# A different passage between two layers of one kernel, and a different order of its beginning

## The chip, the cores and the metric

The kernel runs on one core of a Trainium2 chip. The core has TensorE (PE, matrix products; the loads of its stationary operand are listed as PEld), VectorE (DVE), ScalarE (ACT), GpSimd (POOL) and SyncE (SP), which here only issues transfers. Each engine works through its own instructions in their order and waits for others through semaphores. Sixteen DMA engines move data between the memory outside (HBM) and the core's SBUF. TensorE writes to PSUM, from which VectorE and ScalarE read. The metric is the device time of one execution, in microseconds, and the median of several runs.

## The reference

Two residual layers over `x` of 8 batches, 1024 positions and 512 channels, in float32. The first is attention with weights that are scaled by a condition, the second a gated scan over the positions.

```python
# layer 0: attention
x = x * s1[:, None, :]                                  # s1, s2: halves of the condition
x = (x - mu) * jax.lax.rsqrt(var + EPS_IN)              # over the 512 channels
dcoef = lambda w, s: jax.lax.rsqrt(jnp.einsum('oi,bi->bo', jnp.square(w), jnp.square(s)) + EPS_DM)
q, k, v = (x @ w.T * dcoef(w, s1))                      # v times s2 as well; 16 heads of 32
attn = softmax(q @ k.T * d ** -0.5) @ v
x1 = x_in + attn @ w_weight.T * w_dc + v_flat @ u_weight.T * u_dc
# layer 1: gated scan
xr, gate = jnp.split(x1 @ W_in.T, 2, axis=-1)           # 1024 channels each
xc = silu(conv4(xr + t_emb) + b_conv)                   # along the positions
xn = (xc - mu) / jnp.sqrt(var + 1e-05) * ln_g + ln_b
Bm, Cm, dt = jnp.split(xn @ W_xproj.T, 3, axis=-1)      # 16 states
dt = jnp.tanh(dt @ W_dt.T + b_dt) * 0.01
Ad = 1.0 + dt * A
Bd = Bm * jnp.minimum(norm(xn), 1.0)
h = clip(h * ad + bd * xt, -10, 10);  yt = ct @ h       # 1024 steps, one after the other
out = x1 + (ys + D * xn) * silu(gate) @ W_out.T
```

## The kernel before

The kernel has two functions that run one after the other, and the order of the instructions is written out by hand.

`modulated_attention` first loads and normalises the first batch in two halves of 512 positions (`load_x`, L62; `normalise`, L75 to L89: GpSimd multiplies by the condition and applies mean and deviation, VectorE takes the statistics) and turns it by TensorE transposes so that channels lie on the partitions (`turn`, L99, into tiles `xh`). It then computes the five demodulations: load a weight matrix (L121), square it (L122), multiply by the squared condition in 16 small products per matrix with the weights as the stationary operand (L127), take root and reciprocal (L135, L136). Then `project` computes q, k and v for the first 128 output channels (four heads). A `chain` (L156) is four matrix products that add up in one PSUM tile, and `project` has six of them and two groups of transposes (L202). Copies of q and k shifted by 64 partitions are made by DMA on SP (`moved`, L180 and L181).

The main loop runs over 32 blocks (8 batches of 4 groups of four heads) and in each over 16 slots (8 tiles of 128 queries by 2 pairs of heads). A slot issues: scores (L255, L258), their maxima on VectorE (L363), transposes of the slot before's probabilities (`flip`, L265), exponentials on ScalarE (L373), normalisation on GpSimd (L378, L387, L392), copies out of PSUM, and in every second slot the product with v (`weigh`, L272, with its copy to `aT`, L355). Between these, each slot takes some pieces from a generator, `background`, where a piece is one matrix product of a chain or one group of transposes. `PIECES` paces it. The background of a block is the projection for the next block, and, where they are due, the turning of the next batch, the products `out_w` of the batch before (in blocks 0 and 1 of a batch) and `out_u` (in block 3). Both add to a tile `xr` that is loaded at the start of each chain (L215, L231), `out_u` stores to `xu_d` (L219), `out_w` adds to that and stores to `x1_d` (L235), both outside. A second generator, `aside`, normalises the next batch. After the last slot, `out_w` for the last batch runs by itself (8 chains).

`gated_scan` takes its SBUF from what attention leaves. It loads its weights and constants on SP (L433 to L472), makes three small tables from `w_x`, `w_dt` and the norm's weights (L484, L488, L495), and then follows a `plan`: the scan's step n (L810, one instruction of VectorE per position) and functions put at step numbers. A chunk is 32 positions: products with `W_in` and the convolution (L551 to L578), norm (L596 to L624), a `spill` of the normed rows outside (L628), parameters (L583, L653 to L690, with `spread`, eight small transfers on GpSimd's queue, L672). `fetch` (L776) brings four steps' rows back, each repeated over 16 states: eight transfers of 256 KB on SP per group of four steps. `weigh` in the scan (L786, ScalarE) scales them. The gate, the output product and the store (L764) follow later in the plan. Chunk 0 has the same places relative to its start as the other chunks, at negative numbers.

## Time and profile before

| | us |
|---|---|
| median of 3 runs (lowest, highest) | 5973.01 (5964.13, 5983.14) |
| profiled execution, its time | 5975.06 |
| profiled execution, its span | 5973.3 |
| first score products | 99.50 |
| last `weigh` of attention | 3421.4 to 3423.4 |
| first product of the convolution | 3496.84 |
| first step of the scan | 3552.48 |
| busy: TensorE, VectorE, ScalarE, GpSimd | 5653.9, 4456.9, 3851.8, 1545.8 |

The profile is of one execution. Its page lists busy time per engine, slices of the span, DMA queues, the chain of work that ended last, groups of instructions by line, and DMA issues. Other views give busy time in chosen stretches, the chain in order of time, a timeline, and who waited for whom. An engine's idle time matters only where something on the chain waits for it. TensorE's clock is given as the granted share; at 0.5 a product takes twice as long.

### The profile page before, as it was taken

What the parts mean: (1) busy time and instruction counts of PE and PEld (TensorE: products, weight loads), DVE (VectorE), ACT (ScalarE), POOL (GpSimd) and SP (SyncE); (2) the same over time, 40 slices, a digit from 0 to 9 for tenths busy, and PEclk for the clock granted to TensorE, in tenths of its full rate; (3) what the DMA queues carried; (4) which work ended last, traced back from release to release, by engine and by line L of the source; (5) the groups of instructions that cost most, each with busy time, mean ns of one, the idle gap of its engine ahead of it and who ended that gap; (6) DMA issues with size and microseconds to landing.
All of it is one profiled execution on the core that took longest, in us unless ns stands there. A gap on an engine that the chain in (4) does not pass through costs nothing.

```text
span 5973.3 us, 113397 instructions
## 1 busy us (share of the span) xinstructions
PE 5653.9 (95%) x42960; PEld 3294.2 (55%) x42960; DVE 4456.9 (75%) x6916; ACT 3851.8 (64%) x6743; POOL 1545.8 (26%) x1668
## 2 busy tenths in 40 slices
PE   7999999999999999999999969999999999999998
PEld 4555555556555555555555545555555555555553
DVE  2666666766766666666666649999999999999997
ACT  3555555655655555555555437887888878777886
POOL 2433433433433434334333301111111111111111
PEclk8999999999999999999999989999999999999999
DMA  2102212112112112022111169999999999999997
GB/s 72 38 16 63 56 36 62 38 51 56 33 52 61 26 51 68 19 63 54 40 49 30 49 177 251 248 251 255 255 253 251 253 253 248 244 248 249 253 258 206
DMA packets 387647, 781.80 MB, mean 131 GB/s; under 512 B 203664, under 2 KB 285840, under 8 KB 354336
## 3 DMA queue, kind: packets, MB, share of 16 engines
q1 hardware_dynamic: 358432, 756.07, 47.1%
q0 software_dynamic: 28672, 18.48, 1.3%
q8 instruction: 342, 5.60, 0.4%
q14 instruction: 201, 1.65, 0.1%
HBM read 663.62 MB, written 83.89 MB: 125 GB/s over the span
## 4 chain that ended last, share of the span: by engine, by line
PE 50%; DMA 29%; ACT 8%; DVE 8%; issue 2%; SPq 2%; POOL 0%; DVEq 0%; ACTq 0%; POOLq 0%
DMA xb<-xd 24%; PE mm_ps L156 16%; PE t_ps L265 13%; PE s_ps L255 9%; PE mm_ps L272 8%; DVE h L810 4%; ACT pr L373 3%; DMA xd<-xt 2%; ACT pT L370 2%; SPq L776 2%; DMA x<-x_d 1%; DVE xc L571 1%; ACT xb L786 1%; PE in_ps L551 1%; DVE nmax L363 0%
## 5 line engine op out<-in xcount | busy, mean ns | idle before, releaser
L363 DVE TENSOR_REDUCE nmax<-s_ps 128x1 f32<-128x1024 f32 x1024 | 1205.8, 1219 | 481.2 <-PE s_ps L258 480.5
L370 ACT COPY pT<-t_ps 128x512 f32<-128x512 f32 x1024 | 549.9, 589 | 1380.2 <-PE t_ps L265 1379.9
L810 DVE CUSTOM_DVE_ANT_0 h<-h,xb,lim 128x1024 f32<-128x1024 f32 x1024 | 1372.2, 1340 | 81.4 <-DMA xb<-xd 27.3
L786 ACT ACTIVATE xb<-xb,ws 128x1024 f32<-128x1024 f32 x1024 | 1154.6, 1145 | 193.1 <-DMA xb<-xd 146.0
L265 PEld LDWEIGHTS t_ps<-ident,pr 128*128 128x128 f32 x8192 | 909.8, 141 | 647.2 <-issue 457.0
L373 ACT ACTIVATE pr<-s_ps,nmax 128x1024 f32<-128x1024 f32 x1024 | 1139.7, 1128 | 5.9 <-DVE nmax L363 5.7
L265 PE MATMUL t_ps<-ident,pr 128*128 128x128 f32 x8192 | 1096.1, 277 | 30.8 <-ACT pT L370 28.5
L392 POOL TENSOR_SCALAR pr<-pr,rinv 128x1024 f32<-128x1024 f32 x512 | 572.5, 1118 | 145.7 <-DVE rinv L391 142.6
L255 PE MATMUL s_ps<-kT,qT 32*128 32x512 f32 x2048 | 600.8, 640 | 4.4 <-ACT pr L373 4.4
L797 PE MATMUL y_ps<-h,yw 128*32 128x512 f32 x4096 | 558.2, 601 | 34.8 <-DVE h L810 28.7
L764 POOL DMA_DIRECT2D out<-o_sb x256 | 150.5, 594 | 1701.4 <-ACT few L586 894.2
L258 PE MATMUL s_ps<-k,q 32*128 32x512 f32 x2048 | 577.8, 640 | 0.0
L378 POOL TENSOR_SCALAR pr<-pr,rinv 128x1024 f32<-128x1024 f32 x256 | 286.5, 1119 | 1109.8 <-PE t_ps L265 741.1
L272 PEld LDWEIGHTS mm_ps<-pT,vt 128*32 128x32 f32 x16384 | 438.6, 110 | 235.2 <-issue 94.4
L272 PE MATMUL mm_ps<-pT,vt 128*32 128x128 f32 x16384 | 518.5, 275 | 47.5 <-ACT vt L203 18.5
L387 POOL TENSOR_SCALAR pr<-pr,rinv 128x1024 f32<-128x1024 f32 x256 | 286.3, 1118 | 885.0 <-DVE rinv L386 858.1
L709 PE MATMUL g_ps<-win,x1t 128*128 128x512 f32 x1024 | 488.2, 621 | 1.3 <-DVE xt L609 1.1
L551 PE MATMUL in_ps<-x,win 128*128 128x256 f32 x2048 | 486.2, 380 | 0.0
L749 PE MATMUL o_ps<-wout,xt 128*128 128x512 f32 x1024 | 464.3, 596 | 0.0
L551 PEld LDWEIGHTS in_ps<-x,win 128*128 128x128 f32 x2048 | 386.1, 191 | 89.1 <-issue 32.5
L384 DVE COPY pT<-t_ps 128x512 f32<-128x512 f32 x512 | 351.8, 687 | 77.2 <-PE t_ps L265 76.8
L571 DVE SCALAR_TENSOR_TENSOR xc<-xr,cw,xc 128x256 f32<-128x256 f32 x768 | 368.7, 480 | 20.1 <-ACT xc L564 10.4
(130 smaller groups left out, 6817.5 us busy)
## 6 DMA issues: line engine op xcount, KB each, us to landing
xb<-xd SPq DMA_DIRECT2D x2048, 256.0 KB
xd<-xt SPq DMA_DIRECT2D x64, 512.0 KB
xq<-in_x SPq DMA_DIRECT2D x16, 1024.0 KB
q<-qT SPq DMA_DIRECT2D x128, 128.0 KB
xr<-in_xT SPq DMA_DIRECT2D x64, 256.0 KB
xu_d<-xr SPq DMA_DIRECT2D x64, 256.0 KB
xr<-xu_d SPq DMA_DIRECT2D x64, 256.0 KB
x_d<-xr SPq DMA_DIRECT2D x64, 256.0 KB
```

The lines of the kernel that those rows point to most:

```text
L156: nc.tensor.matmul(ps, w, x, start=(k == 0), stop=(k == KH - 1))
L255: nc.tensor.matmul(s_ps[i][:, 0:HW], st["q"][r, qc], st["k"][r, 0:HW], start=True, stop=True)
L258: nc.tensor.matmul(s_ps[i][:, HW:S], st["q2"][r, qc], st["k2"][r], start=True, stop=True)
L265: nc.tensor.transpose(ps[:, j], pr[:, c0 : c0 + P], ident)
L272: nc.tensor.matmul(av[r], vt[:, kt, r], pT[:, i, kt], start=(kt == 0), stop=(kt == KT - 1), skip_group_check=True,)
L363: nc.vector.tensor_reduce(nmax[i], s_ps[i], AX.X, ALU.max, negate=True)
L370: nc.scalar.copy(pT[:, 0, 4 * g : 4 * g + 4], t_ps[g])
L373: nc.scalar.activation(fresh[i], s_ps[i], AF.Exp, bias=nmax[i], accum_out=rsum[i])
L392: nc.gpsimd.tensor_scalar(fresh[1], fresh[1], rinv[1], 1.0, ALU.mult, ALU.mult)
L551: nc.tensor.matmul(ps, win_sb[:, kk, k * P : (k + 1) * P], st["x1"][:, kk].rearrange("p b t -> p (b t)"), start=(kk == 0), stop=False,)
L786: nc.scalar.mul(xbs[n], xbs[n], sts[c]["ws"][:, t : t + 1])
L810: nc.vector._custom_dve(dve_ops.TENSOR_ADD_SAT, out=h, in0=last["h"], in1=xbs.pop(n), s0=lim[:, 0, t : t + 1], s1=lim[:, 1, t : t + 1],)
```

## The change

The first batch's first half is loaded in two parts with the condition between them; its multiplication moves to VectorE, and ScalarE applies two of the four tiles' mean and deviation. The demodulation of a matrix becomes a generator: four squares, four products with the squared condition as the stationary operand, each into its own 32 partitions, then transposes and a sum. Those of k and q are made before the slots, interleaved with the normalisation; those of v, w and u in the background of block 0. `project` takes a list of steps, so that before the slots only k (both halves) and the first half of q are projected; v, its transposes and the second half of q come in the first slots. `out_u` and `out_w` load `xr` one chain ahead.

The three small tables are made in the background of block 1. At the start of the last block, `handover` loads `W_in` as four tiles of 1 MB into the pools of the batch (`xh`, `xq`). In the last block `out_u` is paced to ten slots and half of the last batch's `out_w` (first 512 positions of all channels) to the last six; the other half runs after the slots. `x1_d` becomes two tensors, one for each half of the positions. The scan loads chunk 0's `x1` and its constants on GpSimd's queue, keeps `xs`, `o_sb` and one `yw` in the batch's pool, and puts what belongs to chunk 0 sixteen places earlier in the plan, and the first three fetches at place -27.

```diff
     def load_x(b, hf):
         xq = tok.tile([P, 4, H], F32, name="xq")
-        nc.sync.dma_start(
-            out=xq, in_=x[b, hf * HW : (hf + 1) * HW].rearrange("(j p) c -> p j c", p=P)
-        )
+        src = x[b, hf * HW : (hf + 1) * HW].rearrange("(j p) c -> p j c", p=P)
+        if b == 0:
+            nc.sync.dma_start(out=xq[:, 0:2], in_=src[:, 0:2])
+        else:
+            nc.sync.dma_start(out=xq, in_=src)
         sr = tok.tile([P, H], F32, name="sr")
         nc.sync.dma_start(out=sr, in_=cond[b, 0:H].unsqueeze(0).to_broadcast([P, H]))
+        if b == 0:
+            nc.sync.dma_start(out=xq[:, 2:4], in_=src[:, 2:4])
         return xq, sr
...
-            nc.gpsimd.tensor_mul(xq[:, j], xq[:, j], sr)
+            (nc.vector if first else nc.gpsimd).tensor_mul(xq[:, j], xq[:, j], sr)
             yield
...
-            nc.gpsimd.tensor_scalar(xq[:, j], xq[:, j], rs[:, j, 0:1], rs[:, j, 1:2], ALU.mult, ALU.add)
+            if first and j % 2 == 0:
+                nc.scalar.activation(xq[:, j], xq[:, j], AF.Identity, bias=rs[:, j, 1:2], scale=rs[:, j, 0:1])
+            else:
+                nc.gpsimd.tensor_scalar(xq[:, j], xq[:, j], rs[:, j, 0:1], rs[:, j, 1:2], ALU.mult, ALU.add)
             yield
...
-    xh_now = []
-    first = [load_x(0, 0), load_x(0, 1)]
-    for xs in first:
-        for _ in normalise(xs):
-            pass
-    for xs in first:
-        for _ in turn(xs, xh_now.append):
-            pass
-    with tc.tile_pool(name="w0", bufs=2) as wp:
-        s2T = wp.tile([P, 2 * KH, B], F32, name="s2T")
-        nc.scalar.activation(s2T, sT, AF.Square)
-        for n, name in enumerate(NAMES):
-            w = wp.tile([P, KH, H], F32, name="w")
-            nc.sync.dma_start(out=w, in_=wT[name].rearrange("(k p) o -> p k o", p=P))
-            nc.scalar.activation(w, w, AF.Square)
...
+    s2T = own.tile([P, 2 * KH, HD], F32, name="s2T")
+    nc.vector.memset(s2T, 0.0)
+    nc.scalar.activation(s2T[:, :, 0:B], sT, AF.Square)
+    def load_full(name, pool, tag):
+        w = pool.tile([P, KH, H], F32, tag=tag, name="w")
+        nc.sync.dma_start(out=w, in_=wT[name].rearrange("(k p) o -> p k o", p=P))
+        return w
+    def demod(ns, ws):
+        for n, w in zip(ns, ws):
+            for k in range(KH):
+                nc.scalar.activation(w[:, k], w[:, k], AF.Square)
+                yield
+            off = 0 if n < 3 else KH
+            d_ps = ps_m.tile([P, H], F32, tag="mm", name="mm_ps")
+            for k in range(KH):
+                nc.tensor.matmul(
+                    d_ps[k * HD : (k + 1) * HD], s2T[:, off + k], w[:, k], start=True, stop=True,
+                    skip_group_check=True,
+                )
+            nc.vector.tensor_copy(w[:, 0], d_ps)
+            yield
+            t_ps = ps_m.tile([P, KH, P], F32, tag="mm", name="mm_ps")
+            for o in range(KH):
+                nc.tensor.transpose(t_ps[:, o], w[:, 0, o * P : (o + 1) * P], ident)
+            nc.vector.tensor_reduce(
+                dc[:, n], t_ps.rearrange("p o (k m) -> p o m k", k=KH)[:, :, 0:B], AX.X, ALU.add
+            )
+            nc.vector.tensor_scalar_add(dc[:, n], dc[:, n], EPS_DM)
+            yield
+        part = dc[:, ns[0] : ns[-1] + 1]
+        nc.scalar.activation(part, part, AF.Sqrt)
+        nc.vector.reciprocal(part, part)
+        if 0 in ns:
+            nc.vector.tensor_scalar_mul(qdc, qdc, float(HD) ** -0.5)
+        if 2 in ns:
+            nc.vector.tensor_mul(vdc, vdc, sT[:, KH : 2 * KH, :])
...
+    STEPS = tuple((name, hf) for hf in range(2) for name in "vktq")
+    def project(ws, xh, b, o, st, steps=STEPS):
...
+    def load_xr(src, o, hf):
+        xr = ring.tile([P, HW], F32, tag="xr", bufs=3, name="xr")
+        nc.sync.dma_start(out=xr, in_=src[o * P : (o + 1) * P, half(hf)])
+        return xr
+        todo = [(o, hf) for o in range(KH) for hf in range(2)]
+        ws, xrs = {0: w0}, {todo[0]: load_xr(xT[b], *todo[0])}
+        for n, (o, hf) in enumerate(todo):
+            c = half(hf)
+            if n + 1 < len(todo):
+                xrs[todo[n + 1]] = load_xr(xT[b], *todo[n + 1])
+            if hf == 0 and o + 1 < KH:
+                ws[o + 1] = load_w("u", o + 1)
+            xr = xrs.pop((o, hf))
...
+    def out_w(b, aTs, todo, w0):
+        ws, xrs = {todo[0][0]: w0}, {todo[0]: load_xr(xu_d[b % 2], *todo[0])}
+        for n, (o, hf) in enumerate(todo):
+            c = half(hf)
+            if n == 0 or todo[n - 1][0] != o:
+                for later, _ in todo[n:]:
+                    if later != o:
+                        ws[later] = load_w("w", later)
+                        break
+            if n + 1 < len(todo):
+                xrs[todo[n + 1]] = load_xr(xu_d[b % 2], *todo[n + 1])
+            xr = xrs.pop((o, hf))
...
+                    out=x1_d[hf][:, :, o, b].rearrange("c p t -> p c t"),
+                    in_=xr.rearrange("p (c t) -> p c t", t=TC),
...
+    xh_now = []
+    first = [load_x(0, 0)]
+    full = {"k": load_full("k", two, "pT")}
+    first.append(load_x(0, 1))
+    wts[0] = {name: load_w(name, 0) for name in "kq"}
+    full["q"] = load_full("q", two, "pT")
+    demods = {name: demod((n,), (full[name],)) for n, name in ((1, "k"), (0, "q"))}
+    for part in (
+        normalise(first[0], True), turn(first[0], xh_now.append), normalise(first[1], True), demods["k"],
+        turn(first[1], xh_now.append), demods["q"],
+    ):
+        for _ in part:
+            pass
+    wts[0]["v"] = load_w("v", 0)
+    demods["v"] = demod((2,), (load_full("v", tok, "xq"),))
+    for _ in project(wts[0], xh_now, 0, 0, sts[0, 0], (("k", 0), ("k", 1), ("q", 0))):
         pass
+    for _ in range(KH):
+        next(demods["v"])
     fetch_w(1)
...
+        if n == 1:
+            tables = early(xp.tile([P, KH * HW], F32, tag="xh", name="tmp"), ps_m)
+            next(tables)
+        if n == 0:
+            yield from demods["v"]
+            yield from project(
+                wts[0], xh_now, 0, 0, sts[0, 0], (("v", 0), ("v", 1), ("t", 0), ("t", 1), ("q", 1))
+            )
+            rest = [load_full(name, tok, "xq") for name in "wu"]
...
+        if n == 0:
+            yield from demod((3, 4), rest)
         if o < 2 and b > 0:
-            yield from out_w(b - 1, [sts[b - 1, k]["a"] for k in range(KH)], 2 * o, 2 * o + 2, w0)
+            yield from out_w(
+                b - 1, [sts[b - 1, k]["a"] for k in range(KH)], [(k, hf) for k in (2 * o, 2 * o + 1) for hf in range(2)], w0
+            )
         if o == KH - 1:
             yield from out_u(b, [sts[b, k]["v"] for k in range(KH)], w0)
+        if n == 1:
+            yield from tables
+        if n == len(blocks) - 1:
+            last_w.append(out_w(
+                b, [sts[b, k]["a"] for k in range(KH)], [(o, hf) for hf in range(2) for o in range(KH)], load_w("w", 0)
+            ))
+            yield
+            for _ in range(4 * KH):
+                yield next(last_w[0])
...
+                if n // SB == len(blocks) - 1:
+                    handover()
...
-            done, pieces = n % SB + 1, PIECES[bo[1]]
+            done, pieces = n % SB + 1, (56, 31)[n // SB] if n < 2 * SB else PIECES[bo[1]]
             few = max(1, (pieces - 2 * NQ + NQ) // SB)
             due = few * (done - done // 2) + -(-(pieces - NQ * few) * (done // 2) // NQ) - ran
+            if n < 3:
+                due = 6
+            if n // SB == len(blocks) - 1:
+                due = -(-33 * min(done, 10) // 10) + 16 * max(done - 10, 0) // 6 - ran
+            due = max(due, 0)
...
-    for _ in out_w(B - 1, [sts[B - 1, k]["a"] for k in range(KH)], 0, KH, load_w("w", 0)):
+    for _ in last_w[0]:
...
+    def work(tmp, psum):
+        wxd, wdt = tmp[0:NS, 0:DI], tmp[0:NS, DI : DI + NS]
+        lg, lb = (tmp[:, DI + NS + n * KI : DI + NS + (n + 1) * KI] for n in range(2))
+        for out, ap in (
+            (wx_sb[:, :, 0 : 2 * NS], w_x.rearrange("(k p) o -> p k o", p=P)), (wxd, w_xd), (wdt, w_dt), (lg, ln_g), (lb, ln_b)
+        ):
+            nc.sync.dma_start(out=out, in_=ap)
+        nc.vector.memset(wx_all[:, KI * NX :], 0.0)
+        yield
+        ps = psum.tile([P, KI, NS], F32, tag="mm", name="mm_ps")
+        for k in range(KI):
+            nc.tensor.matmul(ps[:, k], wxd[:, k * P : (k + 1) * P], wdt, start=True, stop=True)
+        nc.vector.tensor_copy(wx_sb[:, :, 2 * NS : NX], ps)
+        yield
+        for out, v in ((wb, lb), (wgs, lg)):
+            ps = psum.tile([P, NX], F32, tag="mm", name="mm_ps")
+            for k in range(KI):
+                nc.tensor.matmul(
+                    ps, v[:, k : k + 1].to_broadcast([P, P]), wx_sb[:, k, :], start=(k == 0), stop=(k == KI - 1)
+                )
+            nc.vector.tensor_copy(out, ps)
+            yield
+        for k in range(KI):
+            nc.vector.tensor_scalar_mul(wx_sb[:, k, :], wx_sb[:, k, :], lg[:, k : k + 1])
+        yield
...
-    def load(ap, name, shape):
-        t = wp.tile(shape, F32, name=name)
-        nc.sync.dma_start(out=t, in_=ap)
+    def load(ap, name, shape, pool=wp):
+        t = pool.tile(shape, F32, name=name)
+        nc.gpsimd.dma_start(out=t, in_=ap)
         return t
     def load_chunk(c):
-        x1 = two.tile([P, KH, B, TC], F32, bufs=3, name="x1")
-        nc.sync.dma_start(
-            out=x1.rearrange("p k b t -> p (k b t)"), in_=x1_d[c].rearrange("p k b t -> p (k b t)")
+        x1 = x1s.tile([P, KH, B, TC], F32, name="x1")
+        (nc.sync if c > 0 else nc.gpsimd).dma_start(
+            out=x1.rearrange("p k b t -> p (k b t)"),
+            in_=x1_d[2 * c // NCH][c % (NCH // 2)].rearrange("p k b t -> p (k b t)"),
         )
         return x1
-    win_sb = wp.tile([P, KH, 2 * DI], F32, name="win")
-    nc.sync.dma_start(out=win_sb[:, :, 0:DI], in_=w_in[:, 0:DI].rearrange("(k p) o -> p k o", p=P))
     x1_now = load_chunk(0)
+    cond_sb = load(cond, "cond", [P, P])
     cw = load(w_conv.rearrange("(k p) j -> p k j", p=P), "cw", [P, KI, 4])
-    cb = load(cols["b_conv"], "cb", [P, KI])
-    lgb = xtp.tile([P, 2, KI], F32, tag="xt", name="lgb")
-    lg, lb = lgb[:, 0], lgb[:, 1]
-    nc.sync.dma_start(out=lg, in_=cols["ln_g"])
-    nc.sync.dma_start(out=lb, in_=cols["ln_b"])
+    cb = load(b_conv, "cb", [P, KI])
+    bdt = load(b_dt, "bdt", [P, 1])
+    na = load(a_log, "na", [P, 1])
...
+    xs_all = tok.tile([P, KI, CW], F32, tag="xq", name="xs")
+    o_sb = tok.tile([P, H], F32, tag="sr", name="o_sb")
...
+        if args and args[0] is sts[0] and n < -2:
+            n -= 16
...
-            at(p0 + -22, load_x1, st, c)
+            at(p0 + -22 if c > 1 else -34, load_x1, st, c)
...
-        at(4 * g - 9, fetch, g)
+        at(4 * g - 9 if g > 2 else -27, fetch, g)
...
-    x1_d = dram.tile([S // TC, P, KH, B, TC], F32, name="x1_d")
+    x1_d = [dram.tile([S // TC // 2, P, KH, B, TC], F32, name=f"x1_d{n}") for n in range(2)]
...
+    def handover():
+        for k in range(KH):
+            pool, tag = ((xp, "xh"), (tok, "xq"))[k // 3]
+            win.append(pool.tile([P, 2 * DI], F32, tag=tag, name="win"))
+            nc.sync.dma_start(out=win[k], in_=ins["w_in"][k * P : (k + 1) * P])
```

## The prediction

> **What bounds the kernel now.** I read the page's forty slices first, to see where an engine has gaps; then tables of busy time over 20 us windows at the gaps; then the chain of waits and the timeline there; then who waits for the tile `xr`, and the DMA issues.
>
> ```profile
> PE   7999999999999999999999969999999999999998
> DMA  2102212112112112022111169999999999999997
> ...
> 40.00:60.00 20.00, 19.13 (x90) 19.03 (x91) 0.38 (x2) 4.22 (x3) 0.00 (x0) 0.50 0.48 158
> 60.00:80.00 20.00, 13.98 (x44) 10.34 (x45) 1.81 (x5) 1.84 (x2) 0.00 (x0) 0.51 0.14 39
> ...
> 3440.00:3460.00 20.00, 15.91 (x32) 6.02 (x30) 2.25 (x3) 0.00 (x0) 0.00 (x0) 0.91 0.55 115
> 3460.00:3480.00 20.00, 0.03 (x1) 0.00 (x0) 1.63 (x4) 0.00 (x0) 0.00 (x0) 0.55 0.66 190
> ...
> 4000.00:5000.00 1000.00, 966.97 (x4590) 527.95 (x4589) 937.27 (x1357) 811.15 (x1388) 115.99 (x212) 0.99 0.94 253
> ```
>
> The program has two loops: attention until about 3420 us with TensorE full and the DMA engines idle, then the scan with the DMA engines full (0.94, 253 GB/s). TensorE's row drops in the first slice and at the passage (slice 24). In the windows (columns: PE, PEld, DVE, ACT, POOL, clock, DMA share, GB/s) only TensorE works from 40 to 60, at clock 0.50, and nothing from 3460 to 3480. Both gaps are serial, and the loop behind each cannot start sooner: time taken out there should leave the total.
>
> ```profile
> 61.56 7.01 PE mm_ps L127 x32
> 69.60 3.89 DMA w_v<-in_wvT
> 73.84 9.92 PE mm_ps L156 x16
> ...
> 99.61 0.69 ACT qT L184
> 102.70 3.94 DMA w_v<-in_wvT
> ...
> 3423.48 10.51 PE mm_ps L156 x24
> 3434.78 3.76 DMA xr<-xu_d
> ...
> 3486.29 3.56 PE c_ps L484 x16
> 3489.85 3.58 PE wb_ps L488 x16
> 3493.43 3.41 PE wg_ps L495 x16
> 3496.84 3.24 PE in_ps L551 x8
> ```
>
> The chain says what fills the gaps. At the beginning: five demodulations, weights, then six chains of `project`, and the first scores at 99.50. At the passage: eight chains of `out_w`, from the second on each waiting for its `xr`; loads; three tables (10.6 us); the first convolution. The first step of the scan is at 3552.48.
>
> ```profile
>   DMA xr<-xu_d: 33.8, 7
>   DMA xr<-in_xT: 21.4, 7
> ...
> 3304.32 1.18 SPq L164 DMA_DIRECT2D w_u<-in_wuT  x2
> 3315.90 1.02 PE L156 MATMUL mm_ps<-vT,w_u 128*128 128x512 f32 x2
> ...
> out<-o_sb POOLq DMA_DIRECT2D x256, 64.0 KB, 9.6
> bca<-few POOLq DMA_DIRECT2D x256, 6.0 KB, 6.5
> ```
>
> VectorE's idle time before `xr`; the cover between the issue of `w_u` and its use in the last block; and the landing time of the only DMAs that POOL issues now.
>
> **Beginning.** Removed from before the first slot: the demodulations of v, w, u and three of six chains. Worked forward: with half of `xq` loaded before `sr`, `sr` lands some 2.2 us sooner than 8.93 (512 KB at 241 GB/s): 6.8. The four products go to VectorE (half of L641's 1.22 for twice the width, 0.65 with its gap), the last two when the second half is in: 10.2. Statistics 4 x 0.9: 13.8; `rs` 0.9: 14.7; scaling shared by ACT and POOL, two each at 0.76: 16.2; turning 3.9 (28.7 to 32.6 for the second half before): 20.1. Second half the same: 28.5. Demodulation of k: four squares at 0.57 (1.91 for four times the width), the last matmul 1.7 at half clock, copy 0.7, transposes 1.2, reduction, root and reciprocal 1.5: 36. Turning to 39, demodulation of q until its transposes at 45. Three chains, the first at half clock (6.47 for eight records at 73.84), two at 3.6: 58.7. Scaling 0.7, SP issue 1.1, move of `q2` about 3: first scores at 63, for 99.50. That is -36.5. Each further wait between engines costs its 0.2 to 0.5, and twenty of them 10 us (end at 73); all chains at full clock and no wait for `q2`, 55.
>
> Block 0 takes the rest: 56 pieces for 26. A piece of a chain is two records, 0.86; a pair of slots has 7.8 of TensorE without pieces (14.70 with eight). So 62.4 + 36 x 0.86 + 2.4 for transposes + 3 x 4 for demodulations = 108 as TensorE's floor, and 118 if ACT's eight squares in the block (4.6) and two roots between exponentials (two switches each at 1.28, the row of L82's table loads) all show. I take 113; before, 99.5 to 207.1 was 107.6, 6.1 of it a stall for `w_v`. Block 1 spreads 31 pieces evenly and adds 5.4 of tables at full clock (half the 10.6): 8 x 11.2 to 98, I take 97 for 100.2. Loads that it issues on SP: the five of the tables and, later in block 0, `rest`; the q and k moves pass before them, and x of batch 1 waits behind them, needed a slot later. Sum of the beginning: **-34** (-44 to -20).
>
> The page "ScalarE: Activation LUTs", section "What ACT_TABLE_LOAD costs", has about 2.66 us for a switch, drain included, and its rule "Batch activation calls by **set**, not by function" speaks against roots put among exponentials. The trace shows 1.28 for the load; by the page's figure the four switches would cost 10.6 for 5.1, and the total 5.5 more, as an estimate.
>
> **`xr` one chain ahead.** In the blocks the 21.4 of VectorE's waiting may go. A pair with a 2.72 wait took 14.82 for 14.70, one with a 3.33 wait 13.1 for 11.19: mostly hidden by pieces. A weight load on SP now stands one `xr` issue later (0.4). Between 0 and -21.4; by those pairs 0.1 to 1.9 each: **-4**. Next late is the score matmul.
>
> **Last block.** Sixteen pieces of the last output enter it, 13.8 of TensorE. Before, pairs with eight pieces took 14.70 and the last three, without any, 11.19, limited by the exponentials' round trip. Now five pairs with 6.6 (13.5) and three with 5.3 (12.4): 104.6 for 103.6, **+1**: the idle room covers the rest. But `handover` puts 4 MB of `win` on SP, ahead of `w_u`. They can start at about 3304.3 (their buffers fall free with the last q), move at 314 GB/s (3480 to 3500 before) in 13.4, and `w_u` lands near 3321 where it was used at 3315.9. All that stands in TensorE's order behind that matmul waits: transposes, then exponentials. **+5** (0 if transfers are served side by side, 13 if nothing hides it).
>
> **Tail and passage.** After the last weighing (3423.4) four chains remain: 13.8 if nothing is late, 22 at the 5.5 per chain that the old tail shows. The first has its weights and `xr` early; the next wait for a weight buffer set free one chain before, 0.9 to issue and 3.9 to land: I take 17. The win transfer, tables and the half of `x1` that chunk 0 reads are done by then, so `in_ps` starts 17 after 3423.4, where it started 73.2 after: **-56** (-59 to -40).
>
> Cover: x1(0), `cond`, `cw`, `cb` and the other constants now go through POOL's queue, behind POOL's last normalisation at 3419. POOL waits there for the last store of the first half (about 3421), and nothing but loads is queued behind. Its rows show 513 to 594 ns to issue 48 to 64 packets, and 6.5 and 9.6 to land, against 3.8 to 4 for SP's `xr`. Four loads land by 3433 at 0.6 each. `cw`, in 16-byte runs, is 1024 packets, 10 us at 10 ns each: 3443, beside 3440. So it costs 0 to 10, within the -40.
>
> The page "DMA: Bandwidth & Descriptors", section "Issuing engine by pattern", gives simple loads to Sync and calls that path generally faster; its specifications differ by 0.4 us in first byte. By that, x1(0) would be 0.4 later and the sum the same; the rows here differ by more, mixed with other traffic.
>
> **Chunk 0.** Same instructions, 16 plan places earlier. From `in_ps` to the first fetch is 36 us (3496.84 to 3533.09) and to the first step 19 more, one dependent chain. The load of chunk 1's `x1` now stands before the spill on SP (512 KB, 2 us at 253 GB/s), issued long before the spill's data are ready; `spread` stays behind the constants on POOL, some 20 us after the last. Only the first `in_ps`, 3.44 at clock 0.5, falls to 1.7 behind a busy TensorE: **-1** (-4 to +3). At 253 GB/s in the loop the scan's end follows its first fetch; the loop itself I leave at its 2421.
>
> **Sum.** -34 - 4 + 1 + 5 - 56 - 1 = -89. The profiled execution has a span of 5973.3 and took 5975.06, 2 above the median of 5973.01; taking 89 from the span and adding the 1.8 around it gives 5886, from the median 5884: **5885**.
>
> **Rivals.**
>
> *The background does not hide its share.* If squares among exponentials bring table loads (eight squares in eight places with two loads of 1.28 are 20.5) and PSUM's two buffers pass slowly between TensorE and ACT (another 5), the beginning gains 9 and not 34: 5910. For it: the trace shows no square beside an exponential; against it: squares and copies follow the root's load at the begin without another. It would show as table loads in block 0.
>
> *The passage waits for another thing.* `win` ahead of `w_u` at 13, POOL's loads 10 late, the tail at 22, the fetches behind the 2 MB of `wout`: a gain of 20 for 51: 5916. For it: the DMA engines were full whenever weights came; against: they have sixteen idle slots for `win`.
>
> *All on the good side*: scores at 55, no late `w_u`, tail at 13.8, the xr waits gone: -44 - 21 + 1 - 59 - 4 = -127: 5846.
>
> *Slower: the scan's loop pays.* It has 256 groups of four steps at 9.45 us with the DMA engines at 0.94, VectorE at 0.94 and TensorE at 0.97. `xs` and `o_sb` become one tile each for all chunks, and `win` and `xs` lie elsewhere; a new wait on them of 0.35 us per group takes the whole 89, and at 0.45 the time is 6000. Against it: both had one buffer before, so the next chunk already waited for the last reader, and the loop's operations keep their sizes and order.
>
> **How the numbers follow.** 0.55 for the forecast (its own range 5862 to 5905), 0.16 for the first rival, 0.12 for the second, 0.10 for the good side, 0.05 for the slower one, 0.02 for a loss at both places that leaves less than 0.3% (18 us, about what a measurement of this kernel can tell from no change). Faster 0.93, same 0.02, slower 0.05. For 8 in 10 I go from 5850, near the best sum, to 5935: the worst ends of the terms, -20 + 0 + 1 + 13 - 40 + 3 = -43, give 5930.
>
> **What would show it.** First scores near 63; block 0 at 113 with no squares' table loads; the first use of `w_u` in the last block waiting about 5; pairs of that block at 13.5 and 12.4; 17 from the last weighing to `in_ps`; first step near 3480 to 3500; from there to the end as before. Wrong if the span from first step to end moves by over 10 us, if `in_ps` waits for a load of POOL's, or if first scores come after 80.

## The result, and the profile after

| | before | after |
|---|---|---|
| median, us (lowest, highest; runs) | 5974.06 (5964.13, 5983.14; 4) | 5888.38 (5870.31, 5898.99; 4) |
| profiled execution: time, span | 5975.06, 5973.3 | 5898.99, 5896.9 |

After over before is 0.9849, with a 95% interval of 0.9831 to 0.9867: 85.7 us less by the medians, where 89 less than the profiled execution had been forecast (5885). The profiled execution of after is the slowest of its four, so its span fell by only 76.4. The page's slices of after, and its windows of 20 us (columns: PE, PEld, DVE, ACT, POOL, clock, DMA share, GB/s):

```profile
PE   7999999999999999999999989999999999999998
DMA  2112112111112012022111279999999999999997
```

```profile
40.00:60.00 20.00, 16.39 (x45) 5.88 (x44) 4.47 (x8) 7.16 (x12) 0.00 (x0) 0.87 0.25 66
60.00:80.00 20.00, 19.43 (x83) 10.68 (x84) 7.86 (x16) 12.80 (x21) 4.45 (x4) 0.88 0.01 2
3380.00:3400.00 20.00, 19.20 (x193) 11.42 (x192) 9.20 (x17) 5.68 (x12) 9.25 (x12) 1.00 0.46 110
3400.00:3420.00 20.00, 13.21 (x31) 6.37 (x30) 3.37 (x9) 0.60 (x2) 1.19 (x3) 0.83 0.67 172
...
4000.00:5000.00 1000.00, 962.31 (x4554) 522.54 (x4553) 930.14 (x1334) 806.83 (x1377) 116.14 (x212) 1.00 0.93 251
```

The scan's window is as before (0.93 and 251 GB/s for 0.94 and 253). The two gaps are gone: at 60 to 80 the other engines work beside TensorE, and of the passage's gap only a part of 3400 to 3420 is left. The chain of waits of after, at the beginning and at the passage (start, length, what):

```profile
41.80 10.32 PE mm_ps L129 x24
52.14 0.69 ACT qT L206
52.85 2.22 DMA q<-qT
55.12 2.12 PE s_ps L288 x4
...
3271.14 11.70 DMA w_u<-in_wuT
...
3394.60 3.64 PE mm_ps L129 x8
3399.52 8.80 DMA w_w<-in_wwT
3408.45 9.55 PE mm_ps L129 x16
3418.00 1.73 PE in_ps L638 x8
```

Three chains stand before the first scores, where six stood. In the last block `w_u` is waited for behind `W_in`. At the passage two chains run after the last weighing, then the third waits for a tile of `w_w`, and the convolution follows at once, with no loads or tables between.

For the ledger below I read the same points in each trace: the start of the first score product, of the last copy to `aT` of a block (the eighth `weigh`), of the first `in_ps` product, of the issue of the first fetch, and of the first scan step. Us from the span's start (the chain of waits of before lists its first `in_ps` at 3496.84, because the chain counts it from the end of the product ahead of it):

| kernel | first scores | block 0 ends | block 1 ends | blocks 2 to 29 take | last block ends | `in_ps` | first fetch | first step | fetch to end |
|---|---|---|---|---|---|---|---|---|---|
| before | 99.50 | 207.09 | 307.24 | 2919.0 | 3423.51 | 3496.64 | 3533.09 | 3552.48 | 2440.2 |
| after | 52.88 | 177.65 | 276.04 | 2914.5 | 3394.64 | 3417.84 | 3452.82 | 3466.90 | 2444.1 |
| after, again | 51.72 | 171.91 | 271.09 | 2914.5 | 3389.80 | 3413.17 | 3448.16 | 3462.56 | 2434.3 |
| old begin | 95.39 | 202.69 | 303.84 | 2914.7 | 3425.47 | 3448.90 | 3483.9 | 3500.12 | 2449.0 |
| new begin alone | 52.98 | 173.16 | 271.76 | 2922.4 | 3394.01 | 3464.34 | 3501.01 | 3516.8 | 2420.2 |
| `xr` not ahead | 53.50 | 173.70 | 272.76 | 2917.6 | 3394.18 | 3417.74 | 3453.07 | 3468.84 | 2443.8 |
| `W_in` after `w_u` | 51.53 | 171.74 | 270.88 | 2915.0 | 3385.37 | 3408.83 | 3443.83 | 3459.3 | 2439.1 |
| loads on SP | 53.23 | 178.25 | 276.67 | 2914.7 | 3395.24 | 3417.97 | 3454.36 | 3472.89 | 2441.9 |
| `w_w` kept | 53.61 | 176.00 | 274.42 | 2916.4 | 3394.76 | 3408.49 | 3443.68 | 3460.37 | 2434.9 |
| all of `out_w` last | 53.05 | 176.58 | 275.59 | 2914.9 | 3390.99 | 3431.18 | 3466.2 | 3481.53 | 2449.2 |
| broadcasts later | 52.99 | 173.21 | 272.28 | 2917.0 | 3391.35 | 3407.47 | 3442.37 | 3456.76 | 2426.4 |
| `W_in`, `w_w` | 52.90 | 173.10 | 272.23 | 2914.1 | 3385.76 | 3399.49 | 3434.68 | 3449.36 | 2442.5 |
| `W_in`, `w_w`, v | 54.04 | 177.49 | 275.88 | 2916.1 | 3391.45 | 3405.18 | 3440.20 | 3454.45 | 2430.2 |

Two things are to be seen before the experiments. First, after against before ends each stage earlier by -29.4 (block 0), -31.2 (block 1), -35.7 (block 29), -28.9 (last block), -78.8 (`in_ps`), -80.3 (fetch) and -85.6 (first step). Second, the last column lies between 2420 and 2449 over thirteen profiles, and neither its order nor its extremes follow an edit: the changed kernel itself has 2444.1 and 2434.3, and before and the new begin alone, which have the same scan, 2440.2 and 2420.2. Differences of a few us in one total time are therefore read at the first fetch, not at the end.

### The profile page after: what moved, and what is told of

It reads as the page before. It is cut to its first block, busy times and chain, and to the rows that moved or that the text cites. A ratio compares the mean times of both kernels' runs of the same rounds, so it can differ in the third digit from the quotient of the medians.

```text
span 5896.9 us, 113245 instructions
## 1 busy us (share of the span) xinstructions
PE 5607.7 (95%) x42860; PEld 3246.9 (55%) x42860; DVE 4467.2 (76%) x6931; ACT 3861.8 (65%) x6770; POOL 1540.3 (26%) x1667
## 4 chain that ended last, share of the span: by engine, by line
PE 53%; DMA 30%; ACT 7%; DVE 6%; issue 2%; SPq 2%; POOL 0%; DVEq 0%; ACTq 0%; POOLq 0%
DMA xb<-xd 26%; PE mm_ps L129 17%; PE t_ps L295 14%; PE s_ps L285 9%; PE mm_ps L302 8%; ACT pr L450 3%; DVE h L894 3%; DMA xd<-xt 3%; ACT pT L447 2%; SPq L860 2%; DMA x<-x_d 1%; PE in_ps L638 1%; PE g_ps L796 1%; PE y_ps L881 1%; PE o_ps L836 1%
## 5 line engine op out<-in xcount | busy, mean ns | idle before, releaser
L894 DVE CUSTOM_DVE_ANT_0 h<-h,xb,lim 128x1024 f32<-128x1024 f32 x1024 | 1373.0, 1341 | 70.5 <-DMA xb<-xd 24.2
L881 PE MATMUL y_ps<-h,yw 128*32 128x512 f32 x4096 | 571.8, 600 | 44.8 <-DVE h L894 43.9
L302 PE MATMUL mm_ps<-pT,vt 128*32 128x128 f32 x16384 | 515.8, 274 | 41.7 <-ACT vt L223 16.1
L796 PE MATMUL g_ps<-win,x1t 128*128 128x512 f32 x1024 | 471.4, 603 | 1.1 <-DVE xt L696 1.1
L658 DVE SCALAR_TENSOR_TENSOR xc<-xr,cw,xc 128x256 f32<-128x256 f32 x768 | 368.9, 481 | 13.4 <-ACT xc L651 3.6
```

Source lines behind the costliest of these rows:

```text
L302: nc.tensor.matmul(av[r], vt[:, kt, r], pT[:, i, kt], start=(kt == 0), stop=(kt == KT - 1), skip_group_check=True,)
L881: nc.tensor.matmul(st["y", i][32 * r : 32 * r + 32, hf * 512 : (hf + 1) * 512], yws[i][:, 4 * q + r, :], hs[4 * g + r][:, hf * 512 : (hf + ...
L894: nc.vector._custom_dve(dve_ops.TENSOR_ADD_SAT, out=h, in0=last["h"], in1=xbs.pop(n), s0=lim[:, 0, t : t + 1], s1=lim[:, 1, t : t + 1],)
```

## Experiments

The theory was that three places bring the gain, each by its own mechanism: the beginning by work moved behind TensorE's chains, the passage by half of the last output done in the last block and by loads and tables made early, and a little by `xr`; and that these add up.

### Each half of the change by itself

The first kernel is the changed one with the old beginning: five demodulations and all of `project` ahead of the slots. The second is the kernel before with the new beginning and nothing else.

```diff
 # old begin
-    first = [load_x(0, 0)]
-    full = {"k": load_full("k", two, "pT")}
...
+    first = [load_x(0, 0), load_x(0, 1)]
+    for xs in first:
+        for _ in normalise(xs):
+            pass
+    for xs in first:
+        for _ in turn(xs, xh_now.append):
+            pass
+    for n, name in enumerate(NAMES):
+        w = load_full(name, two, "pT")
+        nc.scalar.activation(w, w, AF.Square)
...
-            done, pieces = n % SB + 1, (56, 31)[n // SB] if n < 2 * SB else PIECES[bo[1]]
+            done, pieces = n % SB + 1, (42, 31)[n // SB] if n < 2 * SB else PIECES[bo[1]]
-            if n < 3:
-                due = 6
 # new begin alone, against the changed kernel
-        if n == 1:
-            yield from tables
-        if n == len(blocks) - 1:
-            last_w.append(out_w(
...
-    for _ in last_w[0]:
+    for _ in out_w(B - 1, [sts[B - 1, k]["a"] for k in range(KH)], 0, KH, load_w("w", 0)):
```

> The changed kernel with the beginning of the kernel before: x of batch 0 whole, products on GpSimd, five demodulations and six chains ahead of the first slot, nothing of them in block 0. Theory (serial time at the beginning leaves the total one for one): first scores back at 99.5, the eighth aT copy of block 0 near 207, the time 29 to 31 us above the changed kernel: 5918, ratio to before 0.9905. Rival (the slots of attention take up what the beginning gives, so that the passage holds the whole gain): 5885 to 5895, ratio 0.986. Rival (the passage gains only because attention ends at another point): ratio above 0.993.

> The kernel before with the new beginning alone; xr is loaded at the start of its own chain, the passage is the old one. Theory (the places add up): first scores near 53 to 55, the eighth aT copy of block 0 near 178, of block 1 near 277, and the time 29 to 31 below before: 5944, ratio 0.995. Rival (slots take it up): ratio 0.999 to 1.000.

Measured beside before at 5968.98 (7 runs): with the old begin 5924.44 (5915.65 to 5934.75), ratio 0.9919 (0.9901 to 0.9937); the new begin alone 5938.49 (5923.09 to 5948.56), ratio 0.9945 (0.9926 to 0.9964). The two differences, 44.5 and 30.5, sum to 75.0, where the whole change has 85.7; with intervals of some 11 us on each, they add up as far as can be told. The ledger says it more sharply: the first fetch comes 49.2 earlier with the old begin and 32.1 earlier with the new begin alone, 81.3 together, where the whole change has 80.3 and, in its second profile, 84.9; and from the last copy of attention to `in_ps` it is 23.43 with the old begin and 23.20 in after. So neither half lives on the other, and the new begin alone is worth most of what the forecast gave the beginning (34). Which of the beginning's steps brings how much, no run here takes apart.

### `xr` one chain ahead

```diff
-        ws, xrs = {0: w0}, {todo[0]: load_xr(xT[b], *todo[0])}
+        ws = {0: w0}
...
-            if n + 1 < len(todo):
-                xrs[todo[n + 1]] = load_xr(xT[b], *todo[n + 1])
...
-            xr = xrs.pop((o, hf))
+            xr = load_xr(xT[b], o, hf)
 # and the same in out_w
```

> The changed kernel with xr loaded at the start of its own chain again. Theory (the waits of VectorE for xr are mostly hidden, worth 0.1 to 1.9 us per block 3 of a batch): attention's last aT copy 4 to 6 later than 3394.6, and the tail of four chains longer, each chain 5.3 to 5.5 instead of 3.4 where its weights are there. Rival (the 4.5 us between the two traces in blocks 2 to 29 came from the beginning's shifted order): last aT copy within 1 of 3394.6.

Measured, one run: 5898.76, its first fetch at 3453.07 for 3452.82. What VectorE waits for among the operations on the tile `xr`, of this kernel and then of after (what the wait is for: us, waits):

```profile
  DMA xr<-xu_d: 20.3, 3
  DMA xr<-in_xT: 20.0, 6
```

```profile
  DMA xr<-in_xT: 13.5, 5
```

VectorE's waits for `xr<-xu_d` vanish when it is loaded ahead; those for `in_xT` shrink a little (16.1 in a second profile of after). Blocks 2 to 29 took 2917.6 for 2914.5, and the nine other traces with `xr` ahead lie between 2914.1 and 2917.0. The three traces without it (this one, before, and the new begin alone) lie at 2917.6, 2919.0 and 2922.4, all above. The step is worth about 3 by this experiment, near its 4, and is hardly above the spread; the 4 to 6 of the expectation were not reached. At the passage it brought nothing: without it the tail was 23.56 for 23.20. There its second chain waited 8.42 for `xr`, until 3408.86; in after the third waits 8.80 for a tile of `w_w`, until 3408.32.

### `W_in` behind `w_u`

```diff
-                if n // SB == len(blocks) - 1:
-                    handover()
...
+        if n == SB * (len(blocks) - 1):
+            handover()
```

> The changed kernel with the four loads of win issued after the first slot of the last block, behind the first two w_u and xr. Theory (w_u waits in one queue behind 4 MB of win): the first pair of the last block falls from 18.05 to 12.7 to 13.5, the wait of the first w_u product goes, later xr are one chain ahead and not late, the last aT copy 4.5 to 5.5 earlier relative to the eighth aT copy of block 29. Rival (the stall comes from the block's pieces): the pair stays at 17 to 18. Rival (the stall moves to the xr or w_u behind win): another pair of the block grows by 3 to 5.

Measured, one run: 5884.65, first fetch 3443.83. TensorE's timeline where `w_u` is first used, of after and then of this kernel (start, length, line, tiles, shape, count, idle time before and its cause):

```profile
3282.89 3.04 PE L129 MATMUL mm_ps<-vT,w_u 128*128 128x512 f32 x4 [2.54 <-DMA w_u<-in_wuT]
```

```profile
3275.49 1.88 PE L129 MATMUL mm_ps<-vT,w_u 128*128 128x512 f32 x4
```

In after the product waits 2.54 and then runs slower than full clock (3.04 for 1.88 for the same four). Without the 4 MB ahead of it there is no wait. The first interval between copies to `aT` in the last block, a pair of slots, fell from 18.04 to 13.56, and the other pairs stayed as they were, so what the order of the two loads costs is 4.5: the +5 of the prediction, shown. In the three kernels with this edit that pair took 13.56 each time; in the eight others whose `W_in` goes first it took 16.14 to 18.50.

### Where the passage's 23 come from

The tail was 23.2 for a predicted 17, four chains whose work is 13.8. Three edits take out one suspect each: all four tiles of `w_w` kept from the last block, so that the tail loads no weights; the three constants that are broadcast to all partitions (512 KB each) moved from GpSimd's queue to SP's, behind the tail's weights; and all first loads of the scan on SP.

```diff
 # w_w kept
-        w = ring.tile([P, KH, P], F32, tag=f"w_{name}", name=f"w_{name}")
+        w = ring.tile([P, KH, P], F32, tag=f"w_{name}", bufs=4 if name == "w" else 2, name=f"w_{name}")
...
-                        ws[later] = load_w("w", later)
+                        if later not in ws:
+                            ws[later] = load_w("w", later)
 # broadcasts later
-        nc.gpsimd.dma_start(out=t, in_=ap)
+        (nc.sync if name in ("g_bc", "b_bc", "d_bc") else nc.gpsimd).dma_start(out=t, in_=ap)
 # loads on SP
-        nc.gpsimd.dma_start(out=t, in_=ap)
+        nc.sync.dma_start(out=t, in_=ap)
...
-        (nc.sync if c > 0 else nc.gpsimd).dma_start(
+        nc.sync.dma_start(
```

> The changed kernel with four buffers for w_w, so that the tail's four chains use the weights that the first half loaded. Theory (the tail is late because each chain's weights come one chain ahead): tail 14 to 16 for 23.2, no wait for w_w, full clock. Rival (the tail waits for xr or for x1 through GpSimd's queue just as long): 20 to 23.

> The changed kernel with the three broadcast constants (1.5 MB) on SP behind the tail, x1 and the rest still on GpSimd's queue. Theory (the tail's w_w came late because it shared the DMA engines with these): the wait for w_w falls from 8.8 to 4 to 5, tail 17 to 19, and the centring still finds its constants. Rival (w_w is late for its buffer and for SP's order alone): tail 22 to 24.

> The changed kernel with chunk 0's x1 and all constants of the scan on SP's queue. The tail is measured from the last aT copy to the first convolution product, 23.2 in the changed kernel. Theory (GpSimd's queue serves because SP is held by the tail's stores, which wait for VectorE): x1 is issued only behind the tail's last store, 24 us after the last aT copy and lands 4 later, wout stands ahead of the spill; from the last aT copy to the first fetch 64 to 70 for 58.2, first step 6 to 12 later. Rival (simple loads belong on SP, which is faster): the interval to the first fetch shrinks by 1 to 6, since the tail's weights no longer share with GpSimd's transfers.

Measured, one run each beside before at 5971.67: `w_w` kept 5880.40, broadcasts later 5870.58, loads on SP 5898.07. TensorE's timeline at the tail, of after:

```profile
3394.53 7.13 PE L129 MATMUL mm_ps<-aT,w_w 128*128 128x512 f32 x16
3408.45 9.55 PE L129 MATMUL mm_ps<-aT,w_w 128*128 128x512 f32 x16 [6.79 <-DMA w_w<-in_wwT]
```

of the kernel that keeps `w_w`:

```profile
3394.66 14.00 PE L129 MATMUL mm_ps<-aT,w_w 128*128 128x512 f32 x32
3408.49 1.89 PE L639 MATMUL in_ps<-x,win 128*128 128x256 f32 x8
```

of the kernel with the broadcasts later:

```profile
3391.24 7.13 PE L129 MATMUL mm_ps<-aT,w_w 128*128 128x512 f32 x16
3400.53 7.11 PE L129 MATMUL mm_ps<-aT,w_w 128*128 128x512 f32 x16 [2.15 <-DMA w_w<-in_wwT]
```

and of the one with all loads on SP:

```profile
3404.55 7.11 PE L129 MATMUL mm_ps<-aT,w_w 128*128 128x512 f32 x16 [2.28 <-DMA w_w<-in_wwT]
3417.97 2.50 PE L638 MATMUL in_ps<-x,win 128*128 128x256 f32 x5 [6.32 <-DMA x<-x_d]
```

Without weights to load the tail is 13.73, the prediction's lower bound; so the whole overrun is the tail's weights. With the broadcasts later it is 16.12 and the wait 2.15, with a tile of `w_w` landing in 4.17: two thirds of the wait, and the part clock that follows it (9.55 for 7.11), come from these three transfers beside it. The second profile of after shows the same: 9.35 to land, SP held 6.41. The DMA queues of after from 3395 to 3412 (packets, MB, share of the sixteen engines), and SP's own timeline at the last tile of `w_w`, first in after and then with the broadcasts later:

```profile
q0 software_dynamic: 768, 2.19, 41.6%
q1 hardware_dynamic: 5554, 1.68, 41.2%
```

```profile
3399.52 1.42 SPq L181 DMA_DIRECT2D w_w<-in_wwT  x1
...
3402.95 5.85 SPq L181 DMA_DIRECT2D w_w<-in_wwT  x1
```

```profile
3396.23 1.61 SPq L181 DMA_DIRECT2D w_w<-in_wwT  x1
...
3399.66 1.67 SPq L181 DMA_DIRECT2D w_w<-in_wwT  x1
```

GpSimd's queue (`q0`) holds the same share of the engines as SP's (`q1`), and the load that TensorE waits for takes 8.80 to land; SP itself is held 5.85 at the next one. The Trainium skill, "DMA: Bandwidth & Descriptors", section "Issuing engines are not separate DMA queues", says that transfers started by different engines share the sixteen DMA engines and interleave; these rows agree.

With all loads on SP the wait for `w_w` shrinks too (2.28), but the first half of `x1` now stands in SP's queue behind the tail's stores, and `in_ps` waits 6.32 for it: the first fetch came 1.5 and the first step 6.0 later than in after. So GpSimd's queue is the better place for chunk 0's `x1` in this kernel; the prediction's cover held, and of what goes through GpSimd's queue the three broadcasts are in the wrong place: with them alone moved the wait is 2.15, with everything moved 2.28. The page's section "Issuing engine by pattern", which gives simple loads to Sync, doesn't decide here: what decided for `x1` was what stood ahead of it in SP's queue.

### Half of `out_w` as background

```diff
             yield
-            for _ in range(4 * KH):
-                yield next(last_w[0])
```

> The changed kernel with all eight chains of the last out_w after the slots. Theory (half of them is free in the last block's idle room): the last block's final three pairs fall from 13.0, 13.0 and 10.3 to 11.2 and about 10, that is 3 to 5 in all, the tail grows from 23 to 40 to 48: net loss to the first fetch 13 to 20. Rival (the background costs in the block what it saves behind it): net 0 to 5.

Measured, one run: 5917.41. The chain of waits of this kernel at its tail:

```profile
3395.89 4.07 DMA w_w<-in_wwT
3400.09 3.67 PE mm_ps L129 x8
3403.89 3.69 PE mm_ps L129 x8
3407.60 0.76 DVE xr L266
3408.84 4.17 DMA w_w<-in_wwT
...
3418.11 9.43 DMA w_w<-in_wwT
```

The last block ends 3.65 sooner than in after, the tail takes 40.19 for 23.20, and the first fetch is 13.4 later. Over its last eight pairs alone the block is 3.4 shorter. So four chains that cost 13.8 of TensorE by themselves, and 17.0 in this tail, cost the last block 3.4 to 3.65. Of the passage's 50 (73.13 in before, 23.20 in after) this half is 17.0; the other 33, from loads, tables and `xr` that no longer stand there, no run takes apart.

### The clock in block 0, and a version with three edits

Three more kernels were measured together: after once more; the two edits that paid, `W_in` behind `w_u` and `w_w` kept, together; and these two with v's demodulation, whose root stands between exponentials in slot 0, moved ahead of the slots.

```diff
 # the two edits: the diffs above; v:
-    for _ in project(wts[0], xh_now, 0, 0, sts[0, 0], (("k", 0), ("k", 1), ("q", 0))):
-        pass
-    for _ in range(KH):
-        next(demods["v"])
+    for _ in range(KH):
+        next(demods["v"])
+    for _ in project(wts[0], xh_now, 0, 0, sts[0, 0], (("k", 0),)):
+        pass
+    next(demods["v"])
+    for _ in project(wts[0], xh_now, 0, 0, sts[0, 0], (("k", 1),)):
+        pass
+    for _ in demods["v"]:
+        pass
+    for _ in project(wts[0], xh_now, 0, 0, sts[0, 0], (("q", 0),)):
+        pass
...
-            yield from demods["v"]
...
-            done, pieces = n % SB + 1, (56, 31)[n // SB] if n < 2 * SB else PIECES[bo[1]]
+            done, pieces = n % SB + 1, (54, 31)[n // SB] if n < 2 * SB else PIECES[bo[1]]
-                due = 6
+                due = 5
```

> The changed kernel as it is, beside the two below, so that they can be compared with it and not only with the kernel before. 5880 to 5895 is expected (5888 in its first four runs); first scores at 53, block 0's end at 177, first pair of the last block 18, 23 from the last copy of block 31 to the convolution, first fetch at 3453.

> The changed kernel with the load of W_in behind slot 496's loads of w_u, and all four tiles of w_w kept so that the half after the slots loads no weights again. Each alone gave, up to the convolution: -4.5 in the first pair of the last block, and -9.5 in the products after the slots. Theory: the two places are apart and add up: first pair 13.6, 13.7 from the last copy to the convolution, first fetch at 3439 for 3453, and the time 14 below the changed kernel's of this call (5874 if that is 5888). Rival: the scan, which was 2420 to 2449 long over ten profiles whatever was edited, covers it: then the first fetch is at 3439 and the median differs by less than 7.

> The same two edits, and the demodulation of v taken out of slot 0: its squares ahead of k's first chain, its products between the two chains of k, its root and reciprocal ahead of q's chain. Theory: the two table switches that stood between exponentials and the chain at part half clock leave slot 0: first scores at 56 for 53, slot 0 in 9 to 10 for 13.6, block 0's end 3 to 7 earlier than the changed kernel's, first fetch near 3434, and the time 18 below the changed kernel's of this call. Rival: block 0 is limited by the number of pieces of TensorE's work, so that what leaves slot 0 comes back in the other slots or ahead of it: block 0 ends where it did, and the time is that of the two edits alone.

Measured beside before at 5975.72 (9 runs): after again 5883.22 (5879.21 to 5899.16), ratio 0.985 (0.9834 to 0.9865); two edits 5878.96 (5867.05 to 5901.55), ratio 0.9839 (0.9815 to 0.9862); three edits 5872.82 (5869.54 to 5896.19), ratio 0.9836 (0.9817 to 0.9855).

The two edits add up at the first fetch: 3434.68, 13.5 before after's 3448.16 (14 expected), with 13.6 for the first pair and 13.73 for the tail. In the medians it is 4.3, less than the 7 at which the rival was set, so the rival holds there. The scan took 8.2 more in that profile, and its rate is not the edits' doing; windows of 2000 us of the scan, of after again and then of the two edits:

```profile
3600.00:5600.00 2000.00, 1932.18 (x9161) 1056.76 (x9160) 1870.46 (x2693) 1622.81 (x2767) 229.83 (x420) 0.99 0.94 253
```

```profile
3600.00:5600.00 2000.00, 1919.30 (x9072) 1044.70 (x9071) 1853.72 (x2662) 1610.61 (x2741) 229.87 (x420) 0.99 0.94 250
```

At the same DMA share the engines moved 253 and 250 GB/s, and 2662 operations of VectorE passed for 2693. The changed kernel's own two profiles show both rates (its first had 250). One per cent of the scan is 24 us, more than all that the edits were to bring; so both versions are faster than before, and neither is shown to be faster than after.

Moving v's demodulation gained nothing. The first scores came at 54.04 for 51.72, slots 0 to 2 (each from a slot's second score product to the next slot's) took 24.2 for 26.0, though part of it ran at a lower clock, and slots 3 to 12, at full clock in both, took 66.8 for 64.1: the three pieces fewer in the first slots came back later. That is what the rival, that block 0 is paced by its pieces, had said. The first fetch was 5.5 later than with two edits, but the one profile had a clock of 0.79 and 0.87 from 50 to 70 and 0.83 from 150 to 160, so how much of the 5.5 is the clock's is not shown.

The two profiles of after differ in block 0, from first scores to its end: 124.8 and 120.2. Windows of 10 us, of the first and of the second:

```profile
50.00:60.00 10.00, 7.17 (x21) 1.58 (x19) 2.78 (x3) 5.56 (x9) 0.00 (x0) 0.73 0.50 131
60.00:70.00 10.00, 9.77 (x32) 4.96 (x33) 3.54 (x9) 4.63 (x8) 2.21 (x2) 0.75 0.01 2
```

```profile
50.00:60.00 10.00, 6.06 (x27) 2.02 (x26) 3.43 (x5) 7.64 (x11) 0.00 (x0) 1.00 0.45 121
60.00:70.00 10.00, 9.66 (x47) 5.01 (x46) 4.45 (x10) 6.75 (x12) 4.22 (x4) 1.00 0.00 1
```

The same program had TensorE at 0.73 and 0.75 in one execution, and slot 0, measured so, took 11.4; in the other it had 1.00, and slot 0 took 8.2. In the six traces whose clock was 1.00 throughout block 0 (new begin alone, `xr` not ahead, `W_in` after `w_u`, broadcasts later, two edits, after again) it took 120.2 each time; in the four others with the same block 0 122.4 to 125.0, with 0.72 to 0.88 somewhere between 50 and 70 and in three of them 0.83 from 150 to 160. So 2 to 5 of block 0 come and go with the clock. The Trainium skill, "TensorE: Matmul & The Clock Gate", section "Part 1: The HAM clock gate (the "warmup" mystery)", says that the gate watches activity in a window which runs freely, so that one kernel meets it differently from run to run. These rows agree; no run here shows the window itself. The old beginning has it too: TensorE had 0.50 from 40 to 60 in before and 1.00 with the old begin in the changed kernel, whose first scores came at 95.39 for 99.50:

```profile
40.00:60.00 20.00, 19.49 (x92) 19.40 (x92) 0.57 (x3) 3.82 (x2) 0.00 (x0) 1.00 0.49 162
```

## The prediction, step by step

The total was right, and it was right by terms that were mostly right and by misses that cancelled: the tail's 6 too long against the 5 that were not foreseen ahead of the first step, and, inside the beginning, first scores 10 early against a block 0 that was 7 to 12 too long. That these misses are of one size is luck. The table sets the prediction's terms beside the two profiles of after, each against the one of before:

| term | predicted | after | after, again |
|---|---|---|---|
| beginning, to block 1's end | -34 | -31.2 | -36.2 |
| `xr`, blocks 2 to 29 | -4 | -4.5 | -4.5 |
| last block with `W_in` | +6 | +6.8 | +6.9 |
| tail and passage, to `in_ps` | -56 | -49.9 | -49.8 |
| chunk 0, to first fetch | -1 | -1.5 | -1.5 |
| first fetch to first step | 0 | -5.3 | -5.0 |
| first step to the end | 0 | +9.2 | -0.9 |
| span | -89 | -76.4 | -90.8 |

**Beginning: the sum right, both parts off.** First scores were forecast at 63 (55 to 73) and came at 52.88. Of the 10: the chains began at 41.8 and not 45, they ran in 10.3 and not 13.7, since none had the half clock that I had taken for the first, and behind them the first score product started after 0.8 and not 4.3, since it doesn't need `q2` at all. Scaling and move of `q2` took 3.0, and the half of the scores that needs it began at 55.12; the three terms that the prediction names for this, 0.7, 1.1 and 3, add up to 4.8, so its 63 should have been 63.5. Block 0 took 120.2 at full clock where 113 (108 to 118) was forecast, and 124.8 in the first profile. My upper end had all of ScalarE's squares and switches showing, and this was the nearer one; how the last 2 of the 120.2 arise was not settled. Block 1 took 98.4 and 99.2 for 97, where 100.15 stood before. The first rival's cause, table loads by squares, was refuted: the groups of table loads at the exponentials, of before and then of after, and at the root of the demodulations in after are

```profile
L373 ACT ACT_TABLE_LOAD x15 | 19.2, 1283 | 6.2 <-DVE nmax L363 6.2
L450 ACT ACT_TABLE_LOAD x17 | 21.8, 1283 | 5.6 <-DVE nmax L440 5.5
L170 ACT ACT_TABLE_LOAD x2 | 2.6, 1283 | 0.0
```

with none at the line of the matrices' squares. Two roots and the return to exponentials after each (15 loads stood at the exponentials' line before, 17 now) are the four switches that the prediction had, at 1283 ns each. The longer price of a switch that it also works out was not seen: in slot 0 the copy ahead of a load ends at 69.44, the load takes 69.46 to 70.74, and the exponential starts at 70.75.

**`xr`: right in size, weakly shown.** -4.5 in the profiles, 3 by the experiment, with a spread of about 3 among the traces that load it ahead.

**Last block: right.** The later pairs took 13.0 to 14.3, the last 10.3, where 13.5 and 12.4 were forecast, 1.5 more than before over all eight, and the pair ahead of them, the one in which `w_u` is first used, 5.3 more; that `W_in` ahead of `w_u` is the cause was shown by reversing the two (4.5).

**Tail: the mechanism right, the term mis-sized.** "I take 17" failed, with 23.2, at the sentence that a weight tile needs "0.9 to issue and 3.9 to land". The 3.89 that the prediction shows for such a tile comes from the beginning of before, where the engines had little else to move (a DMA share of 0.14 from 60 to 80). In the tail it took 8.80 beside 1.5 MB of broadcasts, and the next stood 5.85 at issue. The same prediction put those constants on GpSimd with "nothing but loads" queued behind and asked only when they land, not what they take from others; that is the step that was missing. With them moved away the tail is 7.1 shorter, 16.12 and so within the 17, and without the reload 13.7 is reached, my lower bound. The 73.1 from which the term counts is one profile's: the new begin alone, with the old passage, took 70.3, so the passage's gain is 47 to 50. The bound on the cover was too dark: the issue of `cw`, 1024 packets, took 0.92 and not 10, `x1(0)` landed in 3.9, `cw` in 3.4, and no load of GpSimd's gated `in_ps`.

**First step: not foreseen.** 14.1 and 14.4 from fetch to first step for 19.39. The kernel with the new begin alone, which has the old passage, took 15.8, so the new passage isn't needed for most of this gain. With all loads on SP it was 18.5, in the eight other traces 14.3 to 16.7; before has one profile, and the cause was not settled.

**The scan: left at 2421, and that was its good case.** It took 2430.0 and 2419.9 in after. The prediction's test, "Wrong if the span from first step to end moves by over 10 us", sat inside the spread that one kernel shows. The slower rival, a wait in each group of four steps, fell: the changed kernel again took 0.9 less than before from step to end.

## What to carry to other kernels

A serial stretch at the border between two loops was worth its full length here, at the beginning and at the passage, where the loop behind it couldn't start sooner; half of the last output went into the last block at a quarter of its price, where before that block had pairs of 11.2 with, by the prediction's estimate, 7.8 of work for TensorE. When loads are moved early onto another queue, ask what is then loading beside them: here the cost of the early transfers fell on the one that TensorE waited for, not on themselves. Where a loop bound by its transfers varies by one per cent from run to run, as this scan does, read an edit in front of it at the loop's first instruction, and take two profiles of the same kernel before believing a difference of 5 us.

## What the runs showed that was not expected

- The scan's length spreads over 29 us (2420.2 to 2449.2) over thirteen profiles of kernels whose scan differs little or not at all, at DMA rates of 250 to 253 GB/s from 3600 to 5600.
- TensorE's granted clock in one and the same stretch (50 to 70) was 0.74 in one execution of a program and 1.00 in another: 4.6 us in block 0.
- GpSimd took 0.92 to issue `cw`, whose 16 KB are in 16-byte runs, 0.77 for the 512 KB of `x1` and 0.56 for the smallest constants; I had bounded `cw` by 10.
- SP was held 5.85 at one issue of 256 KB, where 1.67 stood without GpSimd's three broadcasts in flight.
